# Attention scores in steps of four PSUM banks instead of two, and maxima found by groups of four heads

## The chip, the core and the metric

The program runs on one core of a Trainium2 chip. A core has TensorE (PE, matmuls; its weight loads are shown as PEld), VectorE (DVE), ScalarE (ACT), GpSimd (POOL) and SyncE (SP, which issues most transfers). Matmuls write into PSUM, which has eight banks of 512 fp32 values for each of 128 partitions; in this kernel only VectorE and ScalarE read them back. The metric is the device time of one execution in microseconds; lower is better.

## The reference, cut to what matters

The model has two layers over x of 4 x 1024 tokens with 256 features: a state-space mixer and an expert layer, then attention and a second expert layer. Each has a layer norm in front and adds its result to x. The change is in the attention and in how its neighbours are cut into pieces:

```python
qkv = jnp.einsum('bsi,oi->bso', x, W_qkv)          # 16 heads of 16
Q, K = (apply_rope(Q), apply_rope(K))
scores = jnp.einsum('bhqd,bhkd->bhqk', Q, K) / jnp.sqrt(jnp.float32(d_k))
scores = jnp.where(causal, scores, -jnp.inf)
attn = jax.nn.softmax(scores, axis=-1)
out = jnp.einsum('bhqk,bhkd->bhqd', attn, V)
```

The second expert layer sends each token to its two best of 16 experts and adds a shared expert.

## The kernel before

**Tiling.** The 4096 tokens are 32 tiles of 128, and four tiles of a batch are a block: 8 blocks, two for each batch. A first block (of a batch) attends to its own 512 keys, a second block to 1024. The blocks are taken in the order 0 to 5, 7, 6. Heads go in four groups of four (`s`); a head takes 32 partitions of the transposed queries `qT` and keys `kT`: 16 dimensions, one extra row, zeros. So a score matmul uses 32 of the 128 rows of the PE array, and matmuls of heads in different row groups can run side by side, each into its own bank.

**Two products.** All scores are computed twice.
- To find each query's maximum (`maxima_of`, "find"): queries as weights, keys moving, out [128 queries x up to 512 keys]; VectorE takes the maximum over the keys, with the causal mask where the tile meets the diagonal (L1485), without it elsewhere (L1489), one instruction for each head. A tile of a second block has two chunks of keys, whose maxima (`part`) are joined by `both_parts` (L1496). The negated maximum goes into the extra column of `qa`, and `renew_steps` turns `qa` again (L1506) and copies it into `qT` (L1510).
- To weigh (`weigh`, "score"): keys as weights, renewed queries moving, out [128 keys x up to 512 queries], already less the maximum; ScalarE takes the exponential into `pt` (L1536), GpSimd clears the part above the diagonal where there is one (`clear`, L1541), and `add` multiplies `pt` with the values, summing over the keys into one bank that is held for the whole head group (`ps_all<-pt,v`).

A find or a score is a step of two heads and two banks: 384 finds and 384 scores. Each takes one half of the array's row groups (`half`), and finds and scores alternate in halves. Finds run 64 ahead of the scores (`AHEAD = 64`); finds go tile by tile, each tile through all 16 heads, and a tile's queries are renewed for all heads at once.

**Other steps.** `norm_steps` adds the first expert layer's rows (L731), normalises a block (statistics in one step of 2.5 us by the planner's costs) and turns it; `project_steps` makes queries, keys and values (`w_qkv`), rotates them (L1392, L1395, L1400); `turn_steps` turns keys and queries (L1429); `end_steps` turns the sums back, normalises and projects them (L1628 to L1652). `routed` chooses the experts. The second expert layer's blocks of rows (`block_steps`, 79 of them) are fetched and sent by GpSimd (L702, L712) and begin in parts after 6, 7 and 8 attention blocks; `shared_steps` is the shared expert.

**What sets the order.** `arranged` plans the order when the program is built. Every step has an engine, a cost in us, banks it takes and gives back, and steps it needs; steps wait in streams, each in its own order. The planner always takes the step that can begin first by its costs, with a handicap for each stream (`Stream(1.9)` and so on) between equals. Each engine gets its instructions in that order and runs them in that order; semaphores hold an instruction until its operands and bank are free. `mm` (L184) issues nearly all matmuls, so lines do not tell them apart, but tiles do: `ps_all<-kT,qT` are finds, `ps_all<-qT,kT` scores.

Of the kernel before, what the change touches and what calls it, by code (L numbers as in the profile page):

```python
# [154 lines left out]
def block_kernel(ctx: ExitStack, tc: tile.TileContext, a, out):  # L155
# [68 lines left out]
    def normalised(gt, tag, pool, v, bufs=1):  # L224

        g, ts = gt
        xs = tiles_of(ts)

        def stats():
            v["st"] = small.tile([P, 4, 6], F32, tag="st", name=f"st_{tag}_{g}")  # L230
            v["mv"] = small.tile([P, 4, 2], F32, tag="mv", name=f"mv_{tag}_{g}")
            for j in range(4):
                nc.vector.bn_stats(v["st"][:, j, :], xs[j])
                nc.vector.bn_aggr(v["mv"][:, j, :], v["st"][:, j, :])
            v["ve"] = small.tile([P, 4], F32, tag="ve", name=f"ve_{tag}_{g}")
            nc.vector.tensor_scalar(v["ve"], v["mv"][:, :, 1], LN_EPS, None, ALU.add)

        def root():
            v["rstd"] = small.tile([P, 4], F32, tag="rstd", name=f"rstd_{tag}_{g}")
            nc.gpsimd.tensor_tensor(v["rstd"], v["ve"], neghalf, ALU.pow)  # L240

        def apply():
            v["xn"] = pool.tile([P, 4, D], F32, tag=f"xn_{tag}", name=f"xn_{tag}_{g}", bufs=bufs)
            for j in range(4):
                nc.vector.tensor_scalar(
                    v["xn"][:, j, :], xs[j], v["mv"][:, j, 0:1], v["rstd"][:, j : j + 1], ALU.subtract, ALU.mult
                )

        return chained([Step(DVE, 2.5, stats, v), Step(POOL, 1.1, root, v), Step(DVE, 1.8, apply, v)])
# [80 lines left out]
    def routed(gt, n_e, w, bias, tag, r, pool, keep=None, part=None):  # L330
# [37 lines left out]
        def choose():  # L368

            lg = v["lg"]  # L370
            mx, ix = sm("mx", [4, 8]), sm("ix", [4, 8], U32)
            for j in range(4):
                nc.vector.max(mx[:, j, :], lg[:, j, :])
                nc.vector.max_index(ix[:, j, :], mx[:, j, :], lg[:, j, :])
            ixf = sm("ixf", [4, 2])
# [61 lines left out]
        def probs():  # L437
# [22 lines left out]
            Step(DVE, 2.65, choose),  # L460
# [8 lines left out]
        kept = steps[2].do  # L469
# [6 lines left out]
        steps[2].do = apply_and_keep  # L476
        if keep is not None:
            copied = steps[5].do
# [5 lines left out]
            steps[5].do = copy_and_keep  # L484
# [759 lines left out]
    for c in range(TPB):  # L1244
# [12 lines left out]
        steps[11].key, steps[16].key, steps[-1].key = ("counted", c + 1), ("chosen", c), ("listed", c + 1)  # L1257
# [12 lines left out]
    for n in range(sum(parts0[-1])):  # L1270
# [21 lines left out]
        "two": [(0, x) for x in combinations(range(NB), 2)],  # L1292
# [18 lines left out]
    qas = [aw.tile([P, NH, 32], F32, name=f"qa_{n}", bufs=1) for n in range(8)]  # L1311
# [18 lines left out]
    before_last = 4 * (len(blocks) - 2) - 1  # L1330
# [10 lines left out]
    def norm_steps(m, v):  # L1341


        def add_rows():
            for n in range(4):
                combine(along(*blocks[m])[1].start + B * n, ygs.pop((m, n)), r0)
            if m + 1 < len(blocks):
# [11 lines left out]
        steps = [Step(DVE, 3.9, add_rows)]  # L1359
# [3 lines left out]
        if m >= 1:  # L1363
            steps[0].need.append(("begun", min(4 * m - 3, before_last)))
        if m >= 2:
            steps[5].need.append(("projected", 4 * m - 5))
            steps[6].need.append(("projected", 4 * m - 5))
        return steps

    def project_steps(n, vn):  # L1370
# [33 lines left out]
        one = Step(PE, 1.9, lambda: product(v, slice(0, 2 * D)), v, take=1, need=[normed])  # L1404
# [6 lines left out]
        if n >= 1:  # L1411
            three.need.append(("added", n - 1))
        if n >= 2:
            one.need.append(("begun", min(n - 2, before_last)))
            four.need.append(("turned", n - 2))
        if n >= len(qas):
            four.need.append(("renewed", n - len(qas)))
        return [one, and_values, three, two, four]

    def turn_steps(n):  # L1420
# [18 lines left out]
        one = Step(PE, 0.55, lambda: turn(0), v[0], take=1, need=[("added", n)])  # L1439
        two = Step(PE, 0.55, lambda: turn(1), v[1], take=1, need=[one], key=("turned", n))  # L1440
# [6 lines left out]
        if n >= 1:  # L1447
            one.need.append(("begun", min(n - 1, before_last)))
        return [one, two, three, four]

    def maxima():


        for m in in_turn:
            for n in range(4 * m, 4 * m + 4):
                t = tiles[n][1]
                chunks = range(0, (t + 1) * P, 512)
                for k0 in chunks:
                    for s in range(NHG):
                        for r in (2, 0):  # L1460
                            key = ("begun", n) if (k0, s, r) == (0, 0, 2) else None
                            yield maxima_of(n, s, r, k0, min((t + 1) * P, k0 + 512), key)

    def maxima_of(n, s, r, k0, k1, key):
        m, j = divmod(n, 4)
        last = k1 == (tiles[n][1] + 1) * P
        nk = k1 - k0

# [6 lines left out]
        def largest(x, banks):  # L1475

            h, ps = 4 * s + r + x, banks[x][:, 0:nk]
            if tiles[n][1] < 4:
                to = qas[n % len(qas)][:, h, DK : DK + 1]
            else:  # L1480
                if n not in parts:
                    parts[n] = small.tile([P, 2, NH], F32, tag="part", name=f"part_{n}")
                to = parts[n][:, k0 // 512, h : h + 1]
            if last:
                nc.vector.tensor_tensor_reduce(  # L1485
                    ps, ps, causal[:, 512 - nk :], -1.0, 3.0e38, ALU.add, ALU.min, accum_out=to
                )
            else:
                nc.vector.tensor_reduce(to, ps, AX.X, ALU.max, negate=True)  # L1489

        end = last and s == NHG - 1 and r == 0
        return dict(n=n, nk=nk, product=product, largest=largest, key=key, end=end, two=tiles[n][1] >= 4)

    def both_parts(n):
        p = parts.pop(n)
        nc.vector.tensor_tensor(qas[n % len(qas)][:, :, DK], p[:, 0, :], p[:, 1, :], ALU.min)  # L1496

    def renew_steps(n):

        m, j = divmod(n, 4)  # L1500
        v = {}

        def turn():
            pt = v["banks"][0].rearrange("p (s t) -> p s t", t=P)
            for s in range(NHG):
                nc.tensor.transpose(pt[:, s, :], qas[n % len(qas)][:, 4 * s : 4 * s + 4, :], ident)  # L1506

        def copy():
            pt = v["banks"][0].rearrange("p (s t) -> p s t", t=P)
            nc.scalar.copy(qTs[m][:, :, j * P : (j + 1) * P], pt)  # L1510

        one = Step(PE, 0.55, turn, v, take=1, need=[("largest", n)], key=("renewed", n))
        return [one, Step(ACT, 0.6, copy, v, give=True, need=[one], key=("ready", n))]

    def weigh(m):
# [5 lines left out]
        for u, (s, k) in enumerate([(s, k) for s in range(NHG) for k in range(nk)]):  # L1521
# [11 lines left out]
            def exp(half, x, w, u=u, lo=lo, v=v):  # L1533
                if half == x == 0:
                    v["pt"] = ak.tile([P, 4, 512], F32, tag="pt", name=f"pt_{m}_{u}")
                nc.scalar.activation(v["pt"][:, 2 * half + x, lo:], w["banks"][x][:, lo:], AF.Exp, scale=DK**-0.5)  # L1536
# [20 lines left out]
            for half in range(2):  # L1557
                w = {}
                two = [
                    Step(ACT, us, lambda half=half, x=x, w=w, exp=exp: exp(half, x, w), w, give=(x,), table="exp")  # L1560
                    for x in range(2)
                ]
                need = [("ready", 4 * m + j) for j in range(4)] if u == 0 and half == 0 else []
# [4 lines left out]
                scores.append(dict(product=score_of, cols=512 - lo, exp=two, w=w, need=need, key=key))  # L1568
# [5 lines left out]
            four = Step(PE, product_us(512 - lo), add, group, take="sum" if k == 0 else None, need=[*exps])  # L1574
# [10 lines left out]

    def together():


        finds, products = list(maxima()), {}
        for i in range(-AHEAD, len(scores)):  # L1590
            if i >= 0:
                of = scores[i]
                w = of["w"]
                do = lambda of=of, w=w: of["product"](w["banks"])
                step = Step(PE, product_us(of["cols"]), do, w, take="two", need=of["need"], key=of["key"], half=i % 2)
                for exp in of["exp"]:
                    exp.need.append(step)
                weighing.add([step])
                products["w", i] = step
                if ("f", i + AHEAD - 1) in products:  # L1600
                    step.need.append(products["f", i + AHEAD - 1])
            if i + AHEAD < len(finds):
                f, v = finds[i + AHEAD], {}
                n = f["n"]
                do = lambda f=f, v=v: f["product"](v["banks"])
                need = [("there", n)] + ([products["w", i - 1]] if i >= 1 else [])
                step = Step(PE, product_us(f["nk"]), do, v, take="two", need=need, key=f["key"], half=1 - i % 2)
                finding.add([step])
                products["f", i + AHEAD] = step
                for x in range(2):  # L1610
                    do = lambda x=x, f=f, v=v: f["largest"](x, v["banks"])
                    largest = Step(DVE, 0.18 + 0.00106 * f["nk"], do, v, give=(x,), need=[step])
                    finding_max.add([largest])
                if f["end"]:
                    if f["two"]:
                        finding_max.add([Step(DVE, 0.2, lambda n=n: both_parts(n), need=[largest])])
                    finding_max.steps[-1].key = "largest", n

    def end_steps(m, i):
# [30 lines left out]
        def add():  # L1650
# [4 lines left out]
            Step(PE, 0.55, turn, v, take=1, need=[("copied", m, s) for s in range(NHG)], key=("out", m, i)),  # L1655
# [3 lines left out]
            Step(PE, 0.95, project, w, key=("projected out", at)),  # L1659
# [120 lines left out]
    def block_steps(n):  # L1780
# [44 lines left out]
        def copy_out():  # L1825
# [5 lines left out]
            Step(PE, 0.3, turn, v, take=1, key=("xb", n)),  # L1831
# [154 lines left out]
```

## Time and profile before

| | |
|---|---|
| median of 15 runs | 1716.95 us (1713.98 to 1721.0) |
| the profiled execution | 1722.56 us, span 1720.4 us, mean granted clock 0.971 |
| PE busy | 1620.0 us (94%) |
| VectorE busy | 988.6 us (57%) |
| ScalarE, GpSimd busy | 698.6 us (41%), 706.5 us (41%) |
| first find, last score on PE | 625.5 us, 1451 us |
| first exponential, last maximum | 717.0 us, 1363.5 us |

Up to 610 us the mixer and the first expert layer run, from 610 to about 1455 us the attention, after that mainly the second expert layer. In the profile an instruction's group is told by line, engine, operation and tiles; "idle before" is the time its engine stood still just ahead of it, with what released it. An fp32 matmul is two records, a transpose one. A matmul's record outlasts the streaming of its columns, so PE's share of busy time says little; starts of one kind of instruction to the start of the next are the better measure.

### The profile page before, as it was taken

The page shows a single profiled execution, that of the slowest core. Times are in us where ns is not written, and L with a number is a line of the kernel's source. Part 1 is how long each engine was busy: PE and PEld are TensorE (multiplying, and loading weights), DVE is VectorE, ACT ScalarE, POOL GpSimd, SP SyncE. Part 2 cuts the span into 40 slices and gives each one's busy share as a digit, 9 for nine tenths or more (in the row PEclk, how much of TensorE's full clock was granted, in tenths as well). Part 3 has the DMA queues.
Part 4 walks back from the last instruction along what each step waited for, and adds up shares of the span by engine and source line. Part 5 has one row for each costly group of instructions (what it writes and reads, how often), then busy time and mean ns, then how long its engine had stood idle before and what let it go on. Part 6 is the DMA issues. An engine that isn't in the chain of part 4 may idle for free.

```text
span 1720.4 us, 32803 instructions
## 1 busy us (share of the span) xinstructions
PE 1620.0 (94%) x11104; PEld 1008.8 (59%) x11104; DVE 988.6 (57%) x3238; ACT 698.6 (41%) x1718; POOL 706.5 (41%) x917
## 2 busy tenths in 40 slices
PE   6999999999999968999999999999999989889994
PEld 3655655799999944545445544455434335667762
DVE  4666655552111167986777777787676615433337
ACT  2334333333333311245554555544555666222220
POOL 2255555566555431121232223133221147677760
PEclk9999999999999977899999999999999999899997
DMA  6000000777666430001010010100002015857758
GB/s 190 13 14 13 14 13 21 233 200 200 206 216 215 154 98 1 25 1 36 16 26 2 25 38 14 25 13 13 14 14 62 13 40 153 190 165 212 213 162 297
DMA packets 121685, 153.55 MB, mean 89 GB/s; under 512 B 17083, under 2 KB 82817, under 8 KB 121490
## 3 DMA queue, kind: packets, MB, share of 16 engines
q1 hardware_dynamic: 100498, 110.13, 21.5%
q0 software_dynamic: 18768, 39.50, 7.6%
q8 instruction: 91, 1.49, 0.4%
q10 hardware_dynamic: 2256, 1.85, 0.4%
q14 instruction: 72, 0.59, 0.2%
HBM read 113.86 MB, written 38.07 MB: 88 GB/s over the span
## 4 chain that ended last, share of the span: by engine, by line
PE 83%; DVE 5%; DMA 5%; issue 3%; POOL 2%; ACT 2%; SPq 0%; POOLq 0%; ACTq 0%; DVEq 0%
PE ps_all L184 75%; DMA y_r_dram<-y_r,out_i_r 3%; PE ps_all L1429 2%; PE ps_all L258 2%; DVE x L731 2%; ACT pt L1536 1%; DVE ps_all L1485 1%; PE ps_all L1506 1%; PE ps_all L1156 1%; PE ps_all L942 1%; PE ps_all L1628 1%; DVE part L1489 1%; POOL y_r_dram L712 1%; POOL xb_r L702 1%; PE ps_all L1790 1%
## 5 line engine op out<-in xcount | busy, mean ns | idle before, releaser
L1536 ACT ACTIVATE pt<-ps_all 128x512 f32<-128x512 f32 (+3 forms) x768 | 320.7, 497 | 248.6 <-PE ps_all L184 244.6
L184 PE MATMUL ps_all<-kT,qT 32*128 32x512 f32 (+3 forms) x1536 | 281.7, 551 | 11.4 <-DVE part L1489 3.6
L1485 DVE CUSTOM_DVE_ANT_0 ps_all<-ps_all,cst 128x512 f32<-128x512 f32 (+3 forms) x512 | 236.7, 523 | 81.1 <-PE ps_all L184 80.7
L184 PE MATMUL ps_all<-qT,kT 32*128 32x512 f32 (+3 forms) x1536 | 262.9, 531 | 2.7 <-ACT pt L1536 1.9
L1541 POOL TENSOR_SCALAR_AFFINE_SELECT pt<-pt 128x512 f32<-128x512 f32 x128 | 81.4, 636 | 343.9 <-ACT pt L1536 343.0
L184 PEld LDWEIGHTS ps_all<-qT,kT 32*128 32x128 f32 x1536 | 105.0, 185 | 131.6 <-ACT pt L1536 45.9
L184 PEld LDWEIGHTS ps_all<-kT,qT 32*128 32x128 f32 x1536 | 125.5, 192 | 94.1 <-ACT pt L1536 33.4
L1489 DVE TENSOR_REDUCE part<-ps_all 128x1 f32<-128x512 f32 x256 | 160.0, 683 | 35.8 <-PE ps_all L184 35.4
L184 PE MATMUL ps_all<-pt,v 128*32 128x512 f32 (+3 forms) x1536 | 164.9, 500 | 8.1 <-POOL pt L1541 7.9
L1183 DVE TENSOR_SCALAR hT<-ps_all,bias_f 128x128 f32<-128x128 f32 x142 | 43.3, 346 | 175.4 <-ACT hT L1185 141.9
L184 PE MATMUL ps_all<-xbT_f,w 128*128 128x128 f32 x1136 | 140.0, 276 | 0.0
L184 PEld LDWEIGHTS ps_all<-xbT_f,w 128*128 128x128 f32 x1136 | 133.2, 192 | 2.1 <-issue 1.3
L184 PE MATMUL ps_all<-w_all,hT 128*128 x568 | 129.8, 381 | 0.0
L184 PE MATMUL ps_all<-xnT_m,w_in 128*128 128x512 f32 x256 | 115.7, 602 | 3.6 <-ACT xnT_m L313 3.6
L184 PEld LDWEIGHTS ps_all<-w_all,hT 128*128 128x128 f32 x568 | 105.1, 190 | 14.3 <-DVE hT L1183 1.6
L712 POOL DMA_INDIRECT y_f_dram<-y_f,out_i_f x71 | 72.7, 1024 | 76.0 <-ACT y_f L1197 58.5
L184 PE MATMUL ps_all<-w_qkv,xnT_a 128*128 128x512 f32 (+1 forms) x256 | 94.9, 514 | 1.3 <-ACT xnT_a L313 1.1
L712 POOL DMA_INDIRECT y_r_dram<-y_r,out_i_r x79 | 79.7, 1009 | 35.9 <-issue 12.8
L184 PE MATMUL ps_all<-xbT_r,wgu 128*128 128x128 f32 x632 | 85.9, 283 | 8.1 <-DMA wgu<-in_Wg_dram 4.1
L702 POOL DMA_INDIRECT xb_r<-xn_dram,in_i_r x79 | 82.4, 1043 | 25.7 <-issue 12.4
L702 POOL DMA_INDIRECT xb_f<-xn_dram,in_i_f x71 | 73.9, 1041 | 39.1 <-PE ps_all L1156 24.2
L184 PEld LDWEIGHTS ps_all<-xbT_r,wgu 128*128 128x128 f32 x632 | 80.0, 196 | 15.8 <-DVE y_r L1827 5.1
(321 smaller groups left out, 2489.9 us busy)
## 6 DMA issues: line engine op xcount, KB each, us to landing
w<-in_w_dram SPq DMA_DIRECT2D x71, 512.0 KB
wgu<-in_Wg_dram SPq DMA_DIRECT2D x79, 128.0 KB
wgu<-in_Wu_dram SPq DMA_DIRECT2D x79, 128.0 KB
yg_f<-y_f_dram SPq DMA_DIRECT2D x32, 256.0 KB
yg_r<-y_r_dram SPq DMA_DIRECT2D x32, 256.0 KB
xn_dram<-xn_f SPq DMA_DIRECT2D x8, 512.0 KB
w_all<-in_w_dram SPq DMA_DIRECT2D x8, 512.0 KB
xn_dram<-xn_r SPq DMA_DIRECT2D x8, 512.0 KB
```

The costliest lines, as they stand in the source:

```text
L184: return nc.tensor.matmul(o, lhsT, rhs, start=start, stop=stop)
L258: nc.tensor.transpose(v["banks"][c][:, j * P : (j + 1) * P], v["xn"][:, j, c * P : (c + 1) * P], ident)
L702: i = nc.gpsimd.indirect_dma_start(xb, None, r["xn"], bass.IndirectOffsetOnAxis(q["in"][:, at : at + 1], 0), bounds_check=NT)
L712: i = nc.gpsimd.indirect_dma_start(r["y"], bass.IndirectOffsetOnAxis(q["out"][:, at : at + 1], 0), y, None, bounds_check=r["y"].shape[0] - 1)
L731: nc.vector.scalar_tensor_tensor(xi, yg[:, k, :], r["pw"][:, t, k : k + 1], xi, ALU.mult, ALU.add)
L942: nc.tensor.transpose(v["banks"][0][:, dc * P : (dc + 1) * P], k["xin"][:, dc, b * P : (b + 1) * P], ident)
L1183: nc.vector.tensor_scalar(to, of, bias, 0.0, ALU.add, ALU.max)
L1429: nc.tensor.transpose(pt[:, s, :], srcs[k][:, 4 * s : 4 * s + 4, :], ident)
L1485: nc.vector.tensor_tensor_reduce(ps, ps, causal[:, 512 - nk :], -1.0, 3.0e38, ALU.add, ALU.min, accum_out=to)
L1489: nc.vector.tensor_reduce(to, ps, AX.X, ALU.max, negate=True)
L1536: nc.scalar.activation(v["pt"][:, 2 * half + x, lo:], w["banks"][x][:, lo:], AF.Exp, scale=DK**-0.5)
L1541: nc.gpsimd.affine_select(d, d, [[0, 4], [1, P]], ALU.is_ge, 0.0, base=0, channel_multiplier=-1)
```

## The change

1. **Steps of four banks.** `side_by_side` pairs finds and scores in one list by a shortest path: a score with a find (in opposite halves of the array), two scores, or two finds, always four matmuls in the four row groups, and a step's cost is its longest product. `together` makes one PE step of each pair that takes four banks together; ScalarE gives back a bank per exponential, VectorE a bank or two. The cost by halves is not used any more.
2. **Finds by groups of heads.** After the first block, finds go head group by head group through the block's four tiles (last tile first), and `renew_steps(m, s)` renews one head group for the whole block: four transposes of the four tiles' `qa`, one copy. `qa` of a block is one tile. A head group's scores may come from 6 finds after its last find (`SLACK`), and have to come before finds are two head groups ahead (`LEAD`), in place of `AHEAD = 64`.
3. **Unmasked maxima of two heads** are one `tensor_reduce` over two banks (128 instructions in place of 256). Masked ones stay one for each head.
4. **Smaller pieces.** The adding of rows and the statistics of a block's norm, and the choice of experts, are cut into steps of one tile or into two; their instructions are the same. Conditions that hold the norm, projection and turning of later blocks back are counted anew (`begun`).
5. **The planner's costs and handicaps** are new throughout the attention.

In the built program each engine has the same instructions as before except for point 3. What changes is their order, from 611 us on; before that, only one copy on VectorE moves. On PE the products now stand in 384 steps of four matmuls, all four of one length: 192 of 512 columns, 64 each of 384, 256 and 128. 308 pair a score with a find, 38 are two finds, 38 two scores. They lie in 265 uninterrupted stretches, 175 of them a single step; before there were 264 stretches, 39 of them a single product of two heads. 12 blocks of the second expert layer are through PE before the last score, 4 before.

```diff
@@ normalised
+        in_pieces = [Step(DVE, 0.62, lambda j=j: stats((j,)), v) for j in range(4)]
+        front = in_pieces if tag in "ar" else [Step(DVE, 2.5, stats, v)]
...
@@ banks
-        "two": [(0, x) for x in combinations(range(NB), 2)],
+        4: [(0, x) for x in combinations(range(NB), 4)],
...
-    qas = [aw.tile([P, NH, 32], F32, name=f"qa_{n}", bufs=1) for n in range(8)]
+    qabs = [aw.tile([P, 4, NH, 32], F32, name=f"qa_{n}", bufs=1) for n in range(2)]
+    qas = [q[:, j] for q in qabs for j in range(4)]
...
@@ maxima
+                turns = [
+                    (n, s, k0)
+                    for s in range(NHG)
+                    for k0 in range(0, 512 * (blk + 1), 512)
+                    for n in reversed(tiles_m)
+                ]
...
             else:
+                one, other = sorted(v["taken"][at : at + 2])
+                assert one == v["taken"][at]
+                ps = ps_all[:, one : other + 1 : other - one, 0:nk]
                 nc.vector.tensor_reduce(to, ps, AX.X, ALU.max, negate=True)
...
@@ renew_steps
-            for s in range(NHG):
-                nc.tensor.transpose(pt[:, s, :], qas[n % len(qas)][:, 4 * s : 4 * s + 4, :], ident)
+            for j in range(4):
+                of = qas[4 * (m % 2) + j][:, 4 * s : 4 * s + 4, :]
+                nc.tensor.transpose(v["banks"][0][:, j * P : (j + 1) * P], of, ident)
...
+            nc.scalar.copy(qTs[m][:, s, :], v["banks"][0])
...
+    def side_by_side(finds):
+        f, w = [x["nk"] for x in finds], [x["cols"] for x in scores]
...
+        earliest = [min(len(f), ends[x["m"], x["s"]] + SLACK) for x in scores]
+        latest = [ends[fours[min(len(fours) - 1, number[x["m"], x["s"]] + LEAD)]] for x in scores]
...
+                if may_w and may_f:
+                    ways.append((1, 1, max(w[i], f[j])))
+                if i % 2 == j % 2 == 0:
+                    if may_w:
+                        ways.append((2, 0, w[i] + 5))
+                    if may_f:
+                        ways.append((0, 2, f[j] + 5))
...
@@ together
-                step = Step(PE, product_us(of["cols"]), do, w, take="two", need=of["need"], key=of["key"], half=i % 2)
...
+            us = max(0.45, 0.06 + 0.00168 * max(x.get("cols", x.get("nk")) for x in of))
+            step = Step(PE, us, do, v, take=2 * len(of), need=[n for x in of for n in x["need"]], key=keys)
...
-    AHEAD = 64
+    SLACK, LEAD = 6, 2
```

## The prediction

> **What bounds the kernel now.** I read the page's slices and chain first, then the stages by windows, then the timeline of PE inside the attention, then that stage's waits.
>
> ```profile
> PE   6999999999999968999999999999999989889994
> DVE  4666655552111167986777777787676615433337
> PEclk9999999999999977899999999999999999899997
> ...
> PE 83%; DVE 5%; DMA 5%; issue 3%; POOL 2%; ACT 2%; SPq 0%; POOLq 0%; ACTq 0%; DVEq 0%
> ...
> 640.00:700.00 60.00, 54.13 (x227) 31.81 (x227) 48.12 (x162) 7.46 (x14) 5.51 (x11) 0.75 0.00 1
> 740.00:1380.00 640.00, 630.46 (x4683) 297.40 (x4683) 475.55 (x1557) 349.32 (x817) 161.22 (x275) 1.00 0.07 21
> 1380.00:1452.00 72.00, 64.97 (x524) 30.74 (x524) 20.64 (x87) 49.83 (x126) 41.68 (x57) 0.95 0.32 87
> ```
>
> The chain is PE's. From 640 to 700 us VectorE is the fuller engine (48.1 of 60) and PE's granted clock is 0.75; from 740 to 1380 PE leads, VectorE is at 74%, ScalarE at 55%; at the end VectorE has nearly nothing left, because finds run 64 ahead. The attention's PE time, first find to the end of the last score, is 625.5 to 1452.3: 826.8 us.
>
> What a product costs is read from starts, in this piece of the timeline:
>
> ```profile
> 1253.57 1.14 PE L184 MATMUL ps_all<-qT,kT 32*128 32x512 f32 x8
> 1254.64 1.06 PE L184 MATMUL ps_all<-pt,v 128*32 128x512 f32 x8
> 1255.64 1.14 PE L184 MATMUL ps_all<-kT,qT 32*128 32x512 f32 x8
> 1256.71 0.64 PE L184 MATMUL ps_all<-xnT_r,wr_sb 128*32 128x256 f32 x8
> 1257.28 1.13 PE L184 MATMUL ps_all<-qT,kT 32*128 32x512 f32 x4
> 1258.34 0.44 PE L355 MATMUL ps_all<-cst,lt_r 128*128 128x128 f32 x2
> ...
> 1228.00 2.07 ACT L1536 ACTIVATE pt<-ps_all 128x512 f32<-128x512 f32 x4 [0.49 <-PE ps_all L184]
> 1243.16 0.64 POOL L1541 TENSOR_SCALAR_AFFINE_SELECT pt<-pt 128x512 f32<-128x512 f32 x1 [1.67 <-ACT pt L1536]
> 1252.29 1.29 DVE L1489 TENSOR_REDUCE part<-ps_all 128x1 f32<-128x512 f32 x2 [0.79 <-PE ps_all L184]
> ...
> PEld ps_all L184 <- ACT pt L1536: 79.6, 160, 0.8
> PEld ps_all L184 <- DVE qa L1485: 23.7, 41, 1.1
> PEld ps_all L184 <- POOL pt L1541: 7.5, 18, 1.4
> ```
>
> Eight records (two steps of two heads, four row groups) take 1.07 us to the next kind of work, four records (one step) take 1.06: a second pair is free, if it stands beside the first. The last three lines are the steady stage's waits: PE's weight loads wait for ScalarE and VectorE to free banks, rarely for GpSimd. Such a wait is not all lost time, as other row groups may still stream.
>
> **The change part by part.**
>
> *Products.* Over 740 to 1380 us, single products take 0.43, 0.64, 0.86 and 1.07 us at 128, 256, 384 and 512 columns, whether of two heads or of four: 0.215 us for each uninterrupted stretch plus 1.667 ns per column. Before, the columns on the busier half of the array, stretch by stretch, add to 173,440, in 264 stretches: 289 + 57 = 346 us. After: 192 x 512 + 64 x (384 + 256 + 128) = 147,456 columns in 265 stretches: 246 + 57 = 303. Gain 43 us, all on the chain.
>
> *What else is on PE.* `pt,v` in unstalled stretches costs 1.00, 0.78, 0.57 and 0.36 us: 149 us for 192, unchanged. All other matmuls up to the last score, at the same kind of price, are 227 us before and 238 after, as 8 more expert blocks come in front. Unstalled sum: before 346 + 149 + 227 = 722, after 690. The trace has 827 for the 722, so 105 us are lost: 43 up to 721 us (start-up) and 62 later (waits).
>
> *Start-up.* Before, the first exponential is at 717, with 64 finds done. After, 24 finds and part of the next come first. VectorE's list up to there, by row: 16 adds 7.4, statistics 5.3, normalising 3.1, seven rotations 9.6, a copy 0.7, masked maxima 16 x (0.26 + 0.39 + 0.52) + 4 x 0.65 = 21.3: 47 us from 611, plus some 10 us in which it waits in the first chain: first exponential near 670. PE's unstalled work by then is about 39 us, so the start-up loses some 12 us (5 to 20) instead of 43.
>
> *Waits.* This decides. A step now needs four banks free at once, of seven (one holds the running sum). I count the need from the timeline: product's end to exponential 0.2, exponentials 0.50 apart at 512 columns, then 0.05 to PE; with a mask 0.13 to GpSimd, 0.63 there, 0.1 to PE. For each first matmul into a bank and each `pt,v` I compared this need with the PE work that stands between in the built order. Shortfalls add up to 115 us before, of which 62 were really lost (a stall also covers later ones); after, to 187: 103 for banks and 84 for `pt,v`, against 94 and 21. The same ratio gives 100. Walking two head groups of second blocks by hand gives 5.0 us lost where little other work stands between the products (group 1 of block 1: two steps back to back want eight banks and wait 0.85; on the diagonal `pt,v` of key tile 4 waits 1.3 for exponential and mask) and 2.8 us where projections and turns fill the gaps (group 0 of block 3); a first block's group, all diagonal, loses about 2.7. With 16 groups of each kind: 16 x 4.1 + 16 x 2.7 = 109. I take 105, and 62 (nothing worse than now) and 150 as ends.
>
> *Two-head maxima.* Two L1489 instructions take 1.29 us; one over 1024 elements should take 1.23 (0.68 plus 512 at the masked rows' slope of 1.06 ns). 128 x 0.06 = 8 us of VectorE, hidden behind PE: 0. Its first bank comes back 0.55 later; the two exponentials of the same step take 1.1 too, so 0, and within the 150 if not.
>
> *Renewal by head group.* Same 128 transposes and 32 copies. Between a group's last find and its transposes 0.2 to 5.6 us of PE work stand, against 1.0 us for two masked maxima of 128, the join and its way: short by 4 us in all, counted in the 105. Scores follow at least 4.7 us later. The smaller pieces of norm and choice are the same instructions in other places on VectorE: 0, covered by the PE work queued ahead of the block that they prepare; if that runs out, a late norm costs at most the 3.9 us that its adds took in one step, for 7 blocks 27.
>
> *Moved expert blocks.* Eight blocks' fetches and sends (L702, L712, about 1.0 us each on POOL, 16 us) and their weight loads on SP now stand ahead of the end of the attention. A `clear` behind a fetch can start 1 us late; POOL is busy 161 of 640, so 0 to +8, taken as 0. After the attention 75 blocks take from 1455 to 1680, 3.0 us each; near the end about 2.7. Eight fewer: -21 (-28 to -10).
>
> *Sum.* 690 + 105 + 12 = 807 against 827, -20; with -21 behind, -41. The profiled execution has 1722.6, so 1681.6; it stands 5.6 above the median, so 1676.
>
> **Two rules weighed.** The row first: four row groups cost 1.07 against 1.06 for two. The Trainium skill, "TensorE: Matmul & The Clock Gate" (Part 3, Measured speedup), gives four row tiles at K = 32 and N = 512 a speedup of 3.07, not 4. As an estimate from that page, a step of four would take 1.30 times as long, the 303 become 394, and the kernel would be some 50 us slower than before. I go by the row. "TensorEngine Tiling (Array Packing)" (PSUM Bottleneck) warns that reading PSUM may become the limit once TensorE is packed; the windows show VectorE at 74% and ScalarE at 55%, so I expect waits for banks, but no full engine.
>
> **Rivals.**
> - *Bank waits eat it (slower).* Above 146 us of waits (0.38 us a step) the gain is gone. For it: 84 us of shortfall at `pt,v` against 21, and a pure stretch before (1226.8 to 1247.8, one head group of a second block) takes 21.0 us with its stalls, while the new one is 20.6 without. Against: the count's ratio. At 165 us: 1742, or 1736 on the median.
> - *Waits stay as they are.* If other work fills the gaps in all groups: 62 in place of 105, 1639, or 1633.
> - *It does not pack more than before.* Where stretches were long, halves already ran side by side; if the 43 are an artefact of my reading and only start-up and waits count, 1681.6 + 43 = 1725, median 1719: no change.
>
> **How the numbers follow.** Forecast (1650 to 1705) 0.58; waits stay 0.20; eaten 0.16; no change 0.06. Ends: 62 of waits, 5 of start-up and -28 behind give 757 and 1625, median 1619; 150, 20 and -10 give 860 and 1745, median 1740. A tenth left out on either side: 1628 to 1728. 0.2%, some 3.4 us, is about what a measurement of this kernel can tell from no change. Faster: 0.58 + 0.20 + 0.04 = 0.82; same 0.04; slower 0.14.
>
> **What would show it.** Products in `x8` stretches with 1.07 from start to start (packing); first exponential near 670 and clock near 1.0 from there (start-up); PE's waits on GpSimd's L1541 grown from 7.5 us several times over, and on ScalarE's L1536 kept or grown (waits); last score near 1432; 12 expert blocks ahead of it and the rest 21 us shorter. Wrong if PE's clock falls below 1.0 in the steady stage, if waits pass 146 us, or if VectorE is over 85% busy there.

## The result: 2.9% slower, and the profile after

The changed kernel takes 1767.95 us (median of 9 runs, 1758.37 to 1771.24), the kernel before 1715.86 beside it: 1.029 times, 95% interval 1.0275 to 1.0306. The forecast was 1676. The profiled execution has 1762.8 us, its span 1761.1.

The page's slices of the changed kernel, then its chain:

```profile
PE   6999999999999789899998999988888899889897
DVE  4666665451111189777487766776466646443337
PEclk9999999999999989999998999989899999999998
...
PE 5%; DMA 4%; issue 2%; POOL 2%; DVE 1%; ACT 0%; SPq 0%; POOLq 0%; DVEq 0%; ACTq 0%
```

The chain breaks off after some 15% of the span, behind the attention, and says nothing of the stage in question. Its stages by windows (length, then busy time of PE, PEld, DVE, ACT and POOL, the granted clock, DMA share, GB/s):

```profile
640.00:700.00 60.00, 56.15 (x349) 28.11 (x348) 54.11 (x172) 22.75 (x54) 14.12 (x24) 0.94 0.12 36
740.00:1380.00 640.00, 570.80 (x4238) 236.79 (x4235) 441.13 (x1292) 317.73 (x727) 145.74 (x243) 0.97 0.07 19
1380.00:1516.00 136.00, 120.79 (x1007) 57.49 (x999) 70.75 (x295) 91.80 (x209) 71.41 (x92) 0.99 0.28 74
```

Between 740 and 1380 us PE is busy 571 of 640 where it was 630, VectorE, ScalarE and GpSimd are less busy than before too, and the clock is 0.97 where it was 1.00. No engine took over. Against the forecast's own terms:

| | forecast | measured |
|---|---|---|
| first find | 625.5, as before | 631.8 |
| unstalled PE work of the attention | 690 | (taken as it is) |
| lost until the first exponential | 12 | 13 (it starts at 677) |
| waits after that (low clock included) | 105 | 181 |
| first find to the start of what follows the last score | 807 | 884.5 (631.8 to 1516.2) |
| behind the attention, against before | -21 | -23 (268 became 245) |

So 76 us of the miss are the waits, 6 the later first find. Of these 6, 3 were there when the stage began (VectorE's first add for it starts at 613.2 instead of 610.3, behind a fetch both times); then PE makes one more set of projections ahead of the first find (2.75 us from 629.1). From the starts of the matmuls, stretch by stretch: products take 469 us where their price is 303, `pt,v` 160 where it is 149, the other matmuls 255 against 238. PE's waits in the steady stage (in all, times, longest):

```profile
PE ps_all L184 <- ACT pt L1566: 40.6, 79, 0.7
PE ps_all L184 <- POOL pt L1571: 9.0, 25, 0.5
PE ps_all L184 <- DVE part L1519: 8.2, 10, 1.6
...
PEld ps_all L184 <- ACT pt L1566: 162.9, 207, 2.3
PEld ps_all L184 <- DVE part L1519: 28.8, 35, 2.2
PEld ps_all L184 <- POOL pt L1571: 28.5, 45, 1.1
```

Two things are in this trace. The first is the timeline of PE with the exponentials beside it:

```profile
1108.00 0.70 PE L184 MATMUL ps_all<-qT,kT 32*128 32x512 f32 x2
1108.01 0.70 PE L184 MATMUL ps_all<-kT,qT 32*128 32x512 f32 x2
1108.53 0.59 PE L184 MATMUL ps_all<-qT,kT 32*128 32x512 f32 x2
1108.54 0.59 PE L184 MATMUL ps_all<-kT,qT 32*128 32x512 f32 x2
1109.07 0.66 PE L1536 MATMUL ps_all<-cst,qa 128*128 128x128 f32 x4
...
1116.13 0.48 PE L184 MATMUL ps_all<-qT,kT 32*128 32x256 f32 x2
...
1116.87 0.66 ACT L1566 ACTIVATE pt<-ps_all 128x256 f32<-128x256 f32 x2 [0.71 <-PE ps_all L184]
1117.30 0.19 PEld L184 LDWEIGHTS ps_all<-qT,kT 32*128 32x128 f32 x2 [0.86 <-ACT pt L1566]
```

A step of four heads alone is as cheap as forecast: 1.07 us from 1108.00 to the next kind of work. But the step at 1116.13 (256 columns, 0.43 us in a run) is followed at once by another; of eight banks one holds the sum, so the second step needs one that the first has filled. It waits until the products are out, some 0.2 us pass, an exponential has run, and starts after 1.17 us. I call this the drain of a step. Against their price, the 209 steps in runs of two and more lost 132 us, 0.63 each; the 175 that stand alone lost 35. Both figures hold every kind of loss, spells of low clock too.

The second is on VectorE, around the two-head maxima (L1519):

```profile
729.62 2.42 DVE L1519 TENSOR_REDUCE part<-ps_all 128x2 f32<-128x1024 f32 x2 [0.49 <-ACT kT L1452]
730.88 0.59 ACT L1452 COPY qT<-ps_all 128x512 f32<-128x512 f32 x1 [1.29 <-DVE part L1519]
733.22 2.36 DVE L1519 TENSOR_REDUCE part<-ps_all 128x2 f32<-128x1024 f32 x2 [1.18 <-PE ps_all L184]
735.63 0.19 PEld L184 LDWEIGHTS ps_all<-qT,kT 32*128 32x128 f32 x2 [3.31 <-DVE part L1519]
735.63 0.70 PE L184 MATMUL ps_all<-qT,kT 32*128 32x512 f32 x2 [2.48 <-DVE part L1519]
737.98 1.22 PE L184 MATMUL ps_all<-kT,qT 32*128 32x512 f32 x2
```

A maximum reads products and nothing else, yet at 729.62 it has waited for a copy of turned keys, and at 730.88 a copy of turned queries has waited for a maximum. Their only common property is the tile of all eight banks. At 735.63 PE has stood still for 2.48 us; matmul records of 512 columns then last 1.22 us instead of 0.6 to 0.7. The experiments stand in the order in which they were made; they led to these rows.

### The profile page after: what moved, and what is told of

Read it like the earlier page. It is cut to its first block, busy times and chain, and to the rows that moved or that the text cites. A ratio compares the mean times of both kernels' runs of the same rounds, so it can differ in the third digit from the quotient of the medians.

```text
span 1761.1 us, 32713 instructions
## 1 busy us (share of the span) xinstructions
PE 1602.2 (91%) x11104; PEld 947.1 (54%) x11104; DVE 997.1 (57%) x3110; ACT 719.7 (41%) x1726; POOL 709.5 (40%) x917
## 5 line engine op out<-in xcount | busy, mean ns | idle before, releaser
L1566 ACT ACTIVATE pt<-ps_all 128x512 f32<-128x512 f32 (+3 forms) x768 | 331.5, 490 | 322.8 <-PE ps_all L184 308.5
L184 PE MATMUL ps_all<-qT,kT 32*128 32x512 f32 (+3 forms) x1536 | 336.7, 544 | 51.4 <-ACT pt L1566 44.6
L184 PE MATMUL ps_all<-kT,qT 32*128 32x512 f32 (+3 forms) x1536 | 338.3, 555 | 7.2 <-DVE part L1519 4.6
L1512 DVE CUSTOM_DVE_ANT_0 ps_all<-ps_all,cst 128x256 f32<-128x256 f32 (+3 forms) x512 | 240.9, 517 | 131.9 <-PE ps_all L184 127.1
L184 PEld LDWEIGHTS ps_all<-qT,kT 32*128 32x128 f32 x1536 | 117.9, 187 | 247.0 <-ACT pt L1566 178.5
L1519 DVE TENSOR_REDUCE part<-ps_all 128x2 f32<-128x1024 f32 x128 | 153.5, 1221 | 85.7 <-PE ps_all L184 75.8
L184 PE MATMUL ps_all<-pt,v 128*32 128x512 f32 (+3 forms) x1536 | 169.8, 512 | 18.0 <-POOL pt L1571 17.2
L184 PEld LDWEIGHTS ps_all<-kT,qT 32*128 32x128 f32 x1536 | 117.3, 188 | 36.2 <-DVE part L1519 18.3
L184 PEld LDWEIGHTS ps_all<-pt,v 128*32 128x32 f32 x1536 | 31.8, 109 | 104.3 <-POOL pt L1571 46.7
```

Of the source, the lines that this page charges most:

```text
L184: return nc.tensor.matmul(o, lhsT, rhs, start=start, stop=stop)
L1512: nc.vector.tensor_tensor_reduce(ps, ps, causal[:, 512 - nk :], -1.0, 3.0e38, ALU.add, ALU.min, accum_out=to)
L1566: nc.scalar.activation(v["pt"][:, 2 * half + x, lo:], of[:, lo:], AF.Exp, scale=DK**-0.5)
```

## Experiments

"Attention" is from the first find's first to the last score's last matmul start: 825.6 us before, 882.5 after. Runs of one group (a, b, c, d, e) share a chip and its runs of the kernel before. That took 1719 us beside group a, but 1794 to 1813 beside the others, whose early stages and last stage are slower; so totals are compared as ratios to the kernel before beside them, and attentions within a group. An attention is read from one profiled execution. The same program gave 854.6, 851.3 and 853.7 (b1, c2, d2) and 788.2 and 790.4 (c4, d3), but the changed kernel 882.5 beside the forecast and 897.1 in group c: differences of a few us say nothing.

### a: are late banks the cause?

```diff
 # a1, a3; a4 the same in the kernel before
+                hi = slice(lo, 512 if m < 2 and u < 8 else lo + P)
...
-                nc.scalar.activation(v["pt"][:, 2 * half + x, lo:], of[:, lo:], AF.Exp, scale=DK**-0.5)
+                nc.scalar.activation(v["pt"][:, 2 * half + x, hi], of[:, hi], AF.Exp, scale=DK**-0.5)
...
 # a2, a3
-                ps = ps_all[:, one : other + 1 : other - one, 0:nk]
+                ps = ps_all[:, one : other + 1 : other - one, 0:P]
...
```

(P is 128. The masked maxima, and in a4 all maxima, are cut to their last 128 columns. For a1, a3 and a4 `pt` has two fixed buffers, which the first exponentials fill whole, so that old values stand in the rest.)

> The changed kernel, every engine's order kept; each exponential reads and writes 128 columns of its bank instead of up to 512 (the outputs are not the reference's), so ScalarE gives a bank of a 512-column step back in about 0.27 us instead of 0.50 to 0.55. Theory A (the order takes four banks at a time and they come back late, from ScalarE and VectorE alike, so each alone hides behind the other): the attention, 884 us from first find to last score, falls by 20 to 50 us, PE's waits on the exponentials shrink from some 200 us to under 80 and those on the maxima grow. Rival B (the four-bank step itself streams slower than 0.215 us + 1.667 ns a column, or the order has too little beside it): under 10 us. Rival C (pt,v waits for the mask on GpSimd): under 10 us.

> The changed kernel, every engine's order kept; each maximum covers 128 columns of its bank instead of up to 512 (two heads at once: 256 instead of 1024; the outputs are not the reference's). Theory A: 20 to 50 us less in the attention, waits on the maxima nearly gone, those on the exponentials kept. Rival B and rival C: under 10 us.

> The changed kernel, every engine's order kept; exponentials and maxima both of 128 columns (the outputs are not the reference's). Theory A: more than the sum of the two alone, 100 to 150 us less in the attention, which comes down to 740 to 780 us against the 690 us without stalls; the granted clock is back at 1.00. Rival B: under 20 us, the product steps keep their 469 us. Rival C: under 30 us, with the waits on GpSimd left.

> The kernel before with the same two cuts (exponentials and maxima of 128 columns; the outputs are not the reference's), its order kept. Theory A: its attention, 827 us, comes down to 740 to 770 us (722 us without stalls), so the 62 us of waits and part of the 43 us of start-up go, and the changed kernel with the cuts is then at or below it, 20 to 50 us faster in total. Rival B: it falls by as much as it has waits, and the changed kernel stays the slower one.

| | ratio to before (95%) | attention |
|---|---|---|
| a1, short exponentials | 1.0095 (1.0063 to 1.0126) | 855.0 |
| a2, short maxima | 0.9966 (0.9954 to 0.9978) | 826.5 |
| a3, both | 0.9729 (0.9692 to 0.9767) | 789.8 |
| a4, both in the kernel before | 0.9697 (0.9657 to 0.9737) | 774.7 |

The steady stage of a3, by windows:

```profile
740.00:1380.00 640.00, 596.17 (x4842) 254.72 (x4839) 321.77 (x1464) 238.38 (x848) 185.05 (x289) 1.00 0.11 27
```

Late banks cost (rival B's "under 10" is out), and the clock is back at 1.00. But theory A failed in three places. The two cuts about add (28 and 56 alone, 93 together) instead of hiding each other, and the maxima are the larger part. PE's waits on the exponentials, foretold at under 80 us in a1, only fell from 203 to 169 in the steady stage. And with both cuts the changed kernel is still no faster than the kernel before with them: its products take 399 us, 96 over their price, 82 of it in runs of steps. The drain also has parts that these cuts leave. Part of a2's gain is the granted clock: counted from its spells at 0.5, it loses 27 us of full speed in the attention of the changed kernel, 26 in a1, 3 in a2 and 2 in a3, so up to 24 of the 56 us.

### b: one part of the change at a time

```diff
 # b1: the same step of the planner, two instructions
-                nc.vector.tensor_reduce(to, ps, AX.X, ALU.max, negate=True)
+                for x in range(2):
+                    ps = v["banks"][at + x][:, 0:nk]
+                    nc.vector.tensor_reduce(to[:, x : x + 1], ps, AX.X, ALU.max, negate=True)
 # b2
-                d = v["pt"][:, :, lo : lo + P]
+                d = v["pt"][:, 0:1, lo : lo + 1]
 # b3, b4
-            us = 0.16 + 0.00083 * (512 - lo)
+            us = 0.11 + 0.00083 * (512 - lo)
-    us = (xs.stop - xs.start) * 0.00104 * x["nk"] + (0.34 if x["last"] else 0.2)
+    us = (xs.stop - xs.start) * 0.00104 * x["nk"] + (0.13 if x["last"] else 0.17)
 # b4
+        cols_of = lambda x: x.get("cols", x.get("nk"))
+        merged = []
         for pair in side_by_side(finds):
+            most = max(cols_of((scores if kind == "w" else finds)[i]) for kind, i in pair)
+            if merged and merged[-1][1] + most <= 512 and len(merged[-1][0]) < 2 * MOST and most == merged[-1][2]:
+                merged[-1] = merged[-1][0] + list(pair), merged[-1][1] + most, most
+            else:
+                merged.append((list(pair), most, most))
...
+    SLACK, LEAD, MOST = 6, 2, 2
...
```

> The changed kernel with one part undone: the unmasked maxima are taken one head at a time again (two instructions of 512 elements for one of 1024), everything else in the same order. Each of the 128 pairs gives its first bank back some 0.55 us earlier and costs VectorE 8 us in all. If late banks are what the attention loses (theory A), and half of PE's 40 to 50 us of waits on the two-head maxima are for a bank of their first head: 5 to 20 us less. If the two-head maxima only save VectorE time, as the prediction had it (0 on the path): within 4 us.

> The changed kernel, same order; the mask on GpSimd clears one element instead of four heads of 128 (the outputs are not the reference's), some 0.2 us instead of 0.64. Theory C (pt,v waits for the mask: the prediction put 84 us of shortfalls there): 20 us or more less. Theory A: what pt,v really lost is 11 us in the attention, and the steps behind it wait for their banks anyway: 3 to 12 us less.

> The changed kernel with two of the planner's prices set to what the trace shows: a masked maximum 0.13 us + 1.04 ns a column instead of 0.34, an exponential 0.11 instead of 0.16 at its start. The work is the same, the planner writes another order. Rival D (the order is bad because its prices were off): 25 us or more faster than the changed kernel. Theory A (any order of four-bank steps with seven banks has the drain of a step on PE's path): within 15 us of it.

> As the one with the measured prices, and two steps of 256 columns, or two of 128, that follow each other share their four banks and are issued as one (324 steps instead of 384, the same columns): 60 drains between steps that stand back to back are gone. Theory A: at 0.5 to 0.7 us each (what such a short step lost in the changed kernel) 30 to 40 us faster than with the prices alone. Theory B (the columns are what costs): within 10 us of it.

| | ratio to before (95%) | attention |
|---|---|---|
| b1, maxima one head at a time | 0.9922 (0.9886 to 0.9958) | 854.6 |
| b2, short mask | 1.0088 (1.0058 to 1.0117) | 893.8 |
| b3, measured prices | 1.0076 (1.0042 to 1.0111) | 883.0 |
| b4, and merged short steps | 0.9975 (0.9941 to 1.0009) | 851.1 |

b1 was the surprise: with two small instructions for one, the rest of the change is a gain. b4 against b3 fits the drain: 60 steps fewer with the same columns are 32 us of attention, 0.53 each, as theory A had it (22 of the total, as the last stage grew by 11). It does not isolate it, since the planner writes another order for the merged steps. The mask (b2, 0.19 us instead of 0.63) and the prices (b3) are not the cause, as both attentions lie between the changed kernel's own, 882.5 and 897.1; without the changed kernel beside them their small effects can't be sized.

### c: the same with the changed kernel beside it

c3 takes b1 and b4 together, with two planner steps for the two maxima. c4 changes the order alone:

```diff
+    FIRST = [56.7, 9.6, -8.4, 6.9, -42.7, ...]
+    for stream, t in zip(streams, FIRST, strict=True):
+        stream.first = t
     in_order(streams, SETS)
```

> The changed kernel itself, as the measure for the three beside it and for the last four, whose chip was slower outside the attention (the stage before it ended some 20 us later, the stage behind it took some 35 us more): 1.029 times the kernel before, its attention 882 us.

> The unmasked maxima one head at a time, all else in the same order, now beside the changed kernel. On the other chip its attention took 855 us. If the two-head maxima are what made the difference (a find's banks come back 0.55 us later, and then the two halves of the next step stream one after the other instead of side by side): 20 to 35 us less than the changed kernel, and the count of steps whose halves stream one after the other falls from 24 to 12. If the other chip made it: within 6 us.

> Measured prices for the planner, maxima one head at a time, and two steps of 256 columns, or two of 128, that follow each other share four banks. Theory A (drains between steps, late banks): the two savings add, 20 to 35 us for the maxima and 20 to 30 for the 60 drains: 40 to 65 us less than the changed kernel, that is 0 to 15 us below the kernel before. Theory B (the columns cost): only the maxima's part.

> As the one before with other handicaps for the attention's streams, found by trying some 1,500 sets against the plan that the kernel's own planner writes; the work is the same. If the order decides how much of the drains other work covers, the attention gets 20 to 30 us shorter than with the old handicaps, below 810 us, and the kernel is 25 to 50 us faster than the kernel before. If drains are there in any order (theory A in its strict form): within 10 us of the one before.

| | ratio to before (95%) | attention | behind it |
|---|---|---|---|
| c1, changed kernel | 1.0165 (1.0127 to 1.0203) | 897.1 | 277 |
| c2, maxima one head at a time | 0.9934 (0.9911 to 0.9956) | 851.3 | 277 |
| c3, and merged short steps | 0.9900 (0.9866 to 0.9934) | 827.9 | 299 |
| c4, and another order | 0.9820 (0.9785 to 0.9854) | 790.4 | 318 |

c1 missed its expectation of 1.029 and 882: on this chip the changed kernel loses less against the kernel before, though its attention is longer. The two-head maxima cost 43 us of the total (1826.0 to 1783.0), more than the 20 to 35 expected, and 46 of the attention: products 480 to 450, other matmuls 257 to 245, `pt,v` 162 to 157. Of the steps that pair a score with a find, 25 had their halves stream one after the other in c1, 12 in c2. That other matmuls gain as well does not fit a find's bank that comes back late; they don't use it. But it is no proof, as they also gain from a clock that is low for less time (37 us of full speed lost in c1, 19 in c2). c3 against c2 is a second measure of merging (with the prices): 23 us for 60 steps fewer, 0.4 each. c4 against c3 is the order alone: 37 us, of which up to 16 are the clock (25 us lost in c3, 9 in c4).

### d: where does the cost sit, and does the order matter?

```diff
 # d1: the kernel before; the first head's step issues nothing
-                nc.vector.tensor_reduce(to, ps, AX.X, ALU.max, negate=True)
+                if x == 1:
+                    to = parts[n][:, k0 // 512, h - 1 : h + 1]
+                    ps = ps_all[:, taken[0] : taken[1] + 1 : taken[1] - taken[0], 0:nk]
+                    nc.vector.tensor_reduce(to, ps, AX.X, ALU.max, negate=True)
```

d2 is b1 again (expected: 0.993 and 850 us), d3 is c4 again, d4 has another set of handicaps.

> The kernel before with one part of the change alone: its unmasked maxima two heads at once, the order of every engine kept. In the changed kernel this part costs 43 us of the total (46 of the attention). If a reduction that holds two banks for 1.2 us is the cost, wherever it stands: 20 us or more slower than the kernel before. If it costs only where PE takes four banks at a time and a find is followed closely by what needs its banks: within 8 us, since here PE takes two at a time and the other half can go on streaming.

> The reordered version again: attention 790 us, 0.982 times the kernel before or less. If the stage behind the attention (318 us there, against 277 for the changed kernel beside it) is paced by transfers that this chip makes faster, it is under 290 us here and the ratio goes to about 0.965; if by the order of the expert blocks, it stays 30 to 40 us longer than that of the one-head version beside it.

> As the reordered version with another set of handicaps, found in the same way. If the order decides the drains, and the plan is a fair guide to it, its attention is within 15 us of 790 again; if the first set was luck, it falls back towards the 828 us of the old handicaps.

| | ratio to before (95%) | attention | behind it |
|---|---|---|---|
| d1, kernel before, maxima of two heads | 1.0887 (1.0831 to 1.0943) | 991.9 | 304 |
| d2, maxima one head at a time | 0.9916 (0.9885 to 0.9946) | 853.7 | 276 |
| d3, reordered | 0.9808 (0.9759 to 0.9858) | 788.2 | 315 |
| d4, another set | 0.9816 (0.9768 to 0.9865) | 800.3 | 303 |

d1 is 152 us slower than the kernel before, where its expectations were 20 or more and less than 8. The low clock is a large part of it (113 us of full speed lost in the attention). Its two-head maxima (line 1492 there), by source: their durations, what they waited for, and who waited for them:

```profile
L1492 DVE TENSOR_REDUCE part<-ps_all x128: 1214/1225/1226, 699.7 to 1476.3; 128x2 f32<-128x1024 f32 x128
...
  PE ps_all L184: 144.9, 72
  ACT pt L1539: 27.0, 14
...
  PEld ps_all L184: 133.3, 77
  PE ps_all L184: 70.3, 58
  ACT pt L1539: 69.7, 32
```

One takes 1.22 us, as forecast, but 128 of them wait 27 us for exponentials, and exponentials 70 us for them. They share no data. The view gives it away: `ps_all[:, one : other + 1 : other - one, 0:nk]` runs from the first bank to the second, and the waits are written as if it touched every bank between. In the built program, 60 of the changed kernel's 128 two-head maxima have banks between their two (84 of d1's 128), and in the changed kernel 34 waits of maxima and 42 waits for maxima are between a maximum and an instruction that uses only a bank in between; in the kernel before and in b1 there is none. The rows around 729.62 are such cases: that maximum reads banks 3 and 6 and waits for the copy out of bank 5, and the copy out of bank 4 waits for it. The product at 735.63 writes bank 1 and has waited for a maximum over banks 0 and 3.

In d3 the attention is 65 us shorter than in d2 (merging, prices and order together), yet the total only 22: of the 79 expert blocks 17 have begun before the last score in d2, 7 in d3, and the blocks behind it take 3.3 and 3.5 us each, so 40 us come back there. With c4, this shows that the order counts, for the waits and for the last stage; the strict form of theory A falls. PE's waits of d3 in the steady stage follow. ScalarE's part, 203 us in the changed kernel and 102 in c3, is 53; VectorE's has grown:

```profile
PEld ps_all L187 <- ACT pt L1568: 49.1, 72, 1.6
PEld ps_all L187 <- DVE part L1520: 44.2, 68, 1.7
...
PE ps_all L187 <- ACT pt L1568: 3.8, 7, 0.8
```

### e: the 128 maxima split by that property

```diff
 # e1; e2 has != instead of ==
+                if other - one == 1:
                     ps = ps_all[:, one : other + 1 : other - one, 0:nk]
                     nc.vector.tensor_reduce(to, ps, AX.X, ALU.max, negate=True)
+                else:
+                    for x in range(2):
+                        ps = v["banks"][at + x][:, 0:nk]
+                        nc.vector.tensor_reduce(to[:, x : x + 1], ps, AX.X, ALU.max, negate=True)
```

> The changed kernel, same order; the unmasked maxima take two heads at once only where the two banks are neighbours (68 of 128), and one head at a time where other banks lie between them (60). Theory E: what costs is that the view of two banks that are not neighbours spans the banks between them, so that the maximum waits for products and exponentials in those banks, and they for it, without sharing data; then this is as fast as the one-head version, 0.990 to 0.996 times the kernel before, attention 848 to 860 us. Theory F: what costs is that a bank comes back 0.55 us later; then some 53% of the 43 us stay, about 1.006, attention near 875.

> The counterpart: two heads at once only where other banks lie between the two (60 of 128), one at a time where they are neighbours. Theory E: as slow as the changed kernel, 1.015 to 1.030 times the kernel before, attention 880 to 900 us. Theory F: some 47% of the 43 us, about 1.004, attention near 872.

e1: 0.9949 (0.9925 to 0.9973), attention 856.4. e2: 1.0186 (1.0133 to 1.0239), attention 909.3, a little above what either theory gave. The clock of the steady stage is 0.98 in e1 and 0.95 in e2; over the attention it loses 22 and 52 us of full speed, so up to 30 of the 53 us between them come by way of the clock. The waits of that stage on the two-head maxima (line 1520), first e1, then e2:

```profile
PEld ps_all L184 <- DVE part L1520: 11.8, 13, 2.2
...
PE ps_all L184 <- DVE part L1520: 3.5, 5, 1.4
```

```profile
PEld ps_all L184 <- DVE part L1520: 25.4, 25, 3.3
...
ACT pt L1571 <- DVE part L1520: 11.7, 4, 8.5
...
PE ps_all L184 <- DVE part L1520: 10.9, 10, 2.5
```

The reductions themselves take the same time over near and distant banks (median 1.22 us in both). But in e2 exponentials wait for them, once for 8.5 us, and in e1 none does. In the built programs e1 has no wait across a bank in between, e2 all those of the changed kernel. So 68 two-head maxima over neighbouring banks cost nothing that shows against b1 (854.6 us on the same chip); 60 over distant banks cost all of it. Theory E holds, theory F falls. The Trainium skill, "PSUM — Partial Sum Buffer" (PSUM bank collisions raise a hardware error), asks for semaphores by bank and quadrant; by that rule a bank in between needs none, and e1 shows that the work runs without these waits.

## Why the prediction was wrong, point by point

- **Two-head maxima, "hidden behind PE: 0": wrong, and the decisive step.** They cost 46 us of attention where they were measured side by side (c1, c2); set against the 882.5 us of the result, the three attentions without them (851 to 855) give 28 to 31. The step counted VectorE's time and the later return of the first bank; duration (1.22 us measured) and that part (nothing that shows, e1 against b1) were right. It never asked which banks the strided view covers, though both the view and the free choice of four banks were in the diff. The waits in between are the cause (e1, e2, and with larger numbers d1), and part of their price is a clock that is low for longer with them.
- **Waits, 105: too small, even without that.** 181 passes the 146 that the prediction named as a sign of error. 181 less 46, or less 28, leaves 135 to 153, near the upper of the forecast's two ends (62 and 150), some of it low clock. The static count of shortfalls was 187; scaling it with the 0.54 that the kernel before had lost is the likely mistake. In a run of steps there is nothing else to stream that would cover a short wait: 209 steps in runs lost 0.63 us each. b4 and c3 fit this (60 fewer steps, 32 and 23 us), but no run shows the ratio by itself. The hand walk's 109 in all came out too small as well.
- **Clock: not forecast.** 0.97 over 640 us is some 20 us, 24 from the first exponential to the last score (the kernel before: 4). It stands inside the 181, not beside it. It was named as a sign of error, and was one.
- **The price of a product: right.** The 109 steps of 512 columns that stand alone have a median of 1.07 us. The estimate of 394 us by "TensorE: Matmul & The Clock Gate" (Part 3) does not fit that row.
- **Start-up: right, its sum not.** 13 us lost instead of 12; the first exponential at 677, 45 us behind the first find. But the 12 does not come out of the prediction's own figures: 670 - 625.5 is 44.5, and less 39 of unstalled work that is 5.5. By the same prices the unstalled work up to there is some 32 us (an estimate from the starts in this trace), so two errors met.
- **`pt,v`: fewer waits than counted.** 84 us of shortfalls, 11 really lost. PE's waits on GpSimd grew as foretold, from 9 to 38 us; with almost no mask (b2) the attention was 893.8 us, between the changed kernel's 882.5 and 897.1.
- **Moved expert blocks: right.** 23 us instead of 21; 17 blocks begun before the last score against 9, the eight counted.
- **Renewal by head group, finds by head group, smaller pieces (0): not taken apart.** No run undoes one of them alone; what they cost is inside the 135 to 153.
- **Rivals.** "Bank waits eat it" gave 165 us of waits and 1736; it came out in sign, with 181 and 1768, but 28 to 46 us of the waits were of a kind that it did not name. Its chance, 0.16, leaned on the ratio 0.54. VectorE, at 69%, never became the bound.

Without the two-head maxima the change is a gain, 0.992 to 0.993 times the kernel before; with merged short steps and another order 0.981 to 0.982, the fastest version of this study.

## What to carry to other kernels

When an operand becomes a strided view over a shared tile, list what lies between its ends, and look in the built program for waits between instructions that share no data; a trace shows them as an engine that waits for one that it has nothing to do with. A ratio of counted to lost waits belongs to the order in which it was measured: when steps get fewer and larger and stand in runs, price the full drain (here some 0.4 to 0.6 us a step). Read the granted clock beside every wait: here part of the price of PE's waits was paid there. Make the part that only saves time on an engine off the path its own run first.

## What was not expected of the hardware

The granted clock falls in steps. A piece of the changed kernel by windows, around PE's 2.48 us gap:

```profile
725.00:735.00 10.00, 7.37 (x48) 3.40 (x48) 8.34 (x10) 2.52 (x5) 1.42 (x2) 1.00 0.00 1
735.00:745.00 10.00, 8.97 (x40) 3.44 (x40) 6.00 (x15) 3.42 (x7) 0.63 (x1) 0.66 0.01 2
745.00:755.00 10.00, 8.54 (x72) 3.62 (x72) 6.93 (x25) 4.17 (x13) 1.90 (x3) 1.00 0.00 1
```

In windows of 1 us the clock is 1.0 or 0.5, apart from those in which it changes, and the spells at 0.5 last multiples of about 3.4 us (3.4 to 13.7 in the changed kernel's attention). The Trainium skill, "TensorE: Matmul & The Clock Gate" (Part 1), gives the same two clocks and a window of about 3.4 us that is judged busy or idle. What the runs add is that gaps shorter than that window are enough: ahead of the seven spells of the changed kernel's attention PE's records show gaps from 0.4 us (a few close together, ahead of 1119.7 or 1232.4) to the one of 2.48 (ahead of 737.4). Most gaps are not followed by a spell (121 of 0.4 us and more, 7 spells), and the runs show no rule that tells which are. The attention of the changed kernel loses 27 us of full clock, that of the kernel before 24, there nearly all of it ahead of the first exponential. From c1 to c2 the loss falls from 37 to 19 us, so up to 18 of the 46 us are the clock, not the waits themselves.
